# Two thirds of the expert slots placed ahead of the last four tiles' routing, which is cut into pieces and laid among them

## The chip, the cores and the metric

The kernel runs on one core of a Trainium2 chip, as one launch. The core has five instruction streams that run at the same time and meet only at semaphores: PE (matrix multiplication), DVE (vector work), ACT (activation functions and copies), POOL (slower vector work, and here the issue of every indirect DMA) and SP (issue of the plain DMAs). Each stream executes its own instructions strictly in order. The metric is the time of one execution in device microseconds (us); of a kernel's runs the median is taken.

## The reference, cut to what matters

A graph of 3,327 nodes with 256 features each (padded to 26 tiles of 128 rows) goes through two layers, every sublayer with a layer norm ahead of it and its result added to x:

```
x = x + gcn(norm(x), adj)          # normalized adjacency times a linear map
x = x + moe(norm(x))               # 8 experts, 2 chosen for each node
x = x + gat(norm(x), adj)          # attention over the graph
x = x + heads(norm(x))             # causal attention with 4 x 4 heads, gates, a small net
```

The change lies in the second line:

```
probs = softmax(tokens @ router_w.T);  rw, re = top_k(probs, 2);  rw = rw / sum(rw)
for e in range(8):
    h = gelu(tokens @ w1[e] + b1[e]);  y = h @ w2[e] + b2[e]
    out = out + combine[:, e:e+1] * y        # only the two chosen experts have a weight
```

## The kernel before, in words

All of it is float32 and written in Tile, a framework that puts instructions in each engine's stream and adds the semaphores. Most stages issue through `InOrder` (L42), a wrapper that keeps each engine's stream in the order in which the Python code makes the calls. Every wrapped call is recorded under line 53, so the profile shows L53 nearly everywhere and is read by tile names.

**The end of the first sublayer.** `graph0` (L151) sums neighbours in two parts. The first 16 row tiles are summed together, in 16 half banks of PSUM. The last ten (the loop over `i` from 16 to 25, L361 on) come one at a time: each takes 26 products of 128x128 by 128x256 in two halves of 13, each half with a panel of the adjacency matrix that SP loads, and ends with `gathered(i)`, a DVE instruction that adds the sum to `x`. After each half, `step(waiting)` (L37) moves every router generator that is under way on to its next `yield`.

**The router.** `Experts.route(tiles)` (L1329) is a generator for a group of tiles. In order it does: statistics of each tile on DVE (`rst`, `rmv`), their power of -0.5 on POOL (`rrs`); the normalized rows `tok` on DVE, and on POOL the sum of `x` and `tok` and a copy of each row's number; transposes on PE and their copy on ACT (`tokt`); logits on PE, softmax and the choice of two experts in some twenty small DVE instructions (`rm`, `rpr`, `ru`, `rat`, `chosen`), with one exponential on ACT; a copy of the first choice into `tok` on POOL; the choices `rsel`, which PE sums over the rows (`before`, `ones`); on DVE the rank of each row within its expert and the row's place in the table `places` in DRAM (`rplace`, which is made in place out of `rat`); and two *puts* per tile (L1437): indirect DMAs, issued by POOL, which scatter the 128 rows of a tile to their places. In the kernel before, tiles 0 to 15 go in four groups of four, tiles 16 to 23 in pairs, tiles 24 and 25 singly; after the last half a plain loop (L376) runs what is left of the generators.

**The experts.** `Experts.run` (L1450) puts 128 rows of zeros behind each expert's rows (8 more puts), then makes from the counts, on DVE, the tables of the 59 *slots*: slot i is 128 rows of one expert, and `row_i`, `exp_i` and `bias` tell which. 59 is what the worst routing needs (two choices times 26 tiles, and 7 for tiles that are not full). Then comes a loop over slots with three of them in work at a time: `take(i + 4)` (L1525) loads a slot's rows from `places` by a DMA of SP, at a row that SP reads from `row_i`; `turn(i)` (L1539) transposes them on PE and copies the expert's first weights and the transposed rows on DVE; `hidden(i - 1)` (L1565) has four products on PE and the gelu on ACT; `result(i - 2)` (L1581) has two products on PE, a DVE addition (`ye`) and a put that scatters the result rows into `made`. At i = 8 some weights for the next sublayer are made in between.

Three rules of order matter for what follows:

- `take` waits for all puts that have been issued by then and that no earlier `take` waited for (`self.puts`, L1529). The list holds the puts into `places` and those into `made`.
- Puts of one group (`places`, `made`) do not wait for each other, since their rows lie apart. A put into `places` is not freed in this way from loads that read `places`: Tile sees a write behind a read of the same tensor.
- POOL issues puts one after another, and everything else that POOL has to do stands in the same stream.

Of the kernel before, what the change touches and what calls it, by code (L numbers as in the profile page):

```python
# [2 lines left out]

# [33 lines left out]
def step(works):  # L37

    works[:] = [w for w in works if next(w, None) is None and w.gi_frame is not None]
# [54 lines left out]
class Net:  # L94
# [56 lines left out]
    def graph0(self, moe):  # L151
# [3 lines left out]
        with ExitStack() as ctx:  # L155
# [198 lines left out]
            moe.open(nc, ctx)  # L354
            coming = [moe.route(range(k, k + 4)) for k in range(0, NI, 4)]
            waiting = []
            H = NT // 2
            for i in range(NI, NT):
                acc = psa.tile([P, 2, D], F32, tag="acc", name="acc")
                for j0 in range(0, NT, H):  # L360
                    pan = panp.tile([P, NI, P], F32, tag="pan", name="pan")  # L361
                    nc.sync.dma_start(out=pan[:, :H, :], in_=a["adjt"][i][:, j0 : j0 + H, :])
                    for j in range(j0, j0 + H):
                        nc.tensor.matmul(
                            acc[:, 0, :], pan[:, j - j0, :], y[:, j, :, :P],
                            start=(j == 0), stop=(j == NT - 1),
                        )
                    if coming:
                        waiting.append(coming.pop(0))
                    step(waiting)  # L370
                gathered(i, acc[:, 0, :])
                if i in (17, 19, 21, 23):
                    coming.append(moe.route(range(i - 1, i + 1)))
                elif i > 23:
                    coming.append(moe.route(range(i, i + 1)))
            while coming or waiting:  # L376
                waiting += coming
                coming = []
                step(waiting)
# [863 lines left out]
class Experts:  # L1243
# [8 lines left out]

    SLOTS = 2 * NT + NE - 1
    ROOM = NP + P
# [54 lines left out]
    def open(self, nc, ctx):  # L1309

        self.nc, a = nc, self.a
        self.ps = ctx.enter_context(
            self.tc.tile_pool(name="mops", bufs=6, space=PSUM, reuse_waits="tile")
# [11 lines left out]

    def bank(self):
        return self.ps.tile([P, 2, D], F32, tag="r", name="rbank")

    def route(self, tiles):  # L1329
# [3 lines left out]
        mv = s.tile([P, 4, 2], F32, tag="rmv", name="rmv")[:, :n, :]  # L1333
        rs = s.tile([P, 4], F32, tag="rrs", name="rrs")[:, :n]
        for i, t in enumerate(tiles):
            st = s.tile([P, 6], F32, tag="rst", name="rst")
            nc.vector.bn_stats(st, x[:, t, :])
            nc.vector.bn_aggr(mv[:, i, :], st)
        nc.vector.tensor_scalar(rs, mv.rearrange("p t s -> p s t")[:, 1, :], 1e-5, None, ALU.add)
        nc.gpsimd.tensor_tensor(rs, rs, net.nhalf[:, :n], ALU.pow)  # L1340
        yield
        toks = []
        for i, t in enumerate(tiles):
            tok = s.tile([P, D + 2], F32, tag="tok", name="tok", bufs=20)
# [3 lines left out]
            toks.append(tok)  # L1348
        for t, tok in zip(tiles, toks):
            nc.gpsimd.tensor_tensor(x[:, t, :], x[:, t, :], tok[:, :D], ALU.add)  # L1350
            nc.gpsimd.tensor_copy(tok[:, D : D + 1], self.leave[:, t : t + 1])
        yield
# [11 lines left out]
        yield  # L1364
# [8 lines left out]
        m = s.tile([P, 4, 2], F32, tag="rm", name="rm")[:, :n, :]  # L1373
        pr = s.tile([P, 4, NE], F32, tag="rpr", name="rpr")[:, :n, :]
        u = s.tile([P, 4, NE], F32, tag="ru", name="ru")[:, :n, :]
# [4 lines left out]
        iota = self.iota.unsqueeze(1).to_broadcast([P, n, NE])  # L1380
        nc.vector.tensor_reduce(m[:, :, 0], pl, AX.X, ALU.max)
        nc.vector.tensor_tensor(pr, pl, wide(m[:, :, 0]), ALU.subtract)
        yield
        nc.scalar.activation(pr, pr, AF.Exp)
        yield
        nc.vector.tensor_reduce(m[:, :, 0], pr, AX.X, ALU.add)
        nc.vector.reciprocal(m[:, :, 0], m[:, :, 0])
        nc.vector.tensor_tensor(pr, pr, wide(m[:, :, 0]), ALU.mult)

        at = s.tile([P, 4, 2], F32, tag="rat", name="rat")[:, :n, :]  # L1390
        for k in range(2):
# [3 lines left out]
            nc.vector.scalar_tensor_tensor(u, u, float(NE), iota, ALU.mult, ALU.add)  # L1395
            nc.vector.tensor_reduce(at[:, :, k], u, AX.X, ALU.min)
            nc.vector.tensor_tensor(oh, iota, wide(at[:, :, k]), ALU.is_equal)
            if k == 0:
                nc.vector.scalar_tensor_tensor(pr, oh, -2.0, pr, ALU.mult, ALU.add)
        for i in range(n):  # L1400
            nc.gpsimd.tensor_copy(toks[i][:, D + 1 :], at[:, i, 0:1])
        sel = s.tile([P, 4, NE], F32, tag="rsel", name="rsel")[:, :n, :]
# [3 lines left out]
        w = s.tile([P, 4], F32, tag="rw", name="rw")[:, :n]  # L1406
        nc.vector.tensor_tensor(w, m[:, :, 0], m[:, :, 1], ALU.add)
        nc.vector.tensor_scalar(w, w, 1e-12, None, ALU.max)
        nc.vector.reciprocal(w, w)
# [3 lines left out]
        yield  # L1413
# [7 lines left out]
        whole = pc[:, 0, ds(n * NE, n * NE)].rearrange("p (t e) -> p t e", e=NE)  # L1421
        for i in range(n):
            nc.vector.tensor_tensor(u[:, i, :], above[:, i, :], self.count, ALU.add)
            nc.vector.tensor_tensor(self.count, self.count, whole[:, i, :], ALU.add)
        for k in range(2):
            nc.vector.tensor_tensor(pr, u, self.chosen[:, t0 : t0 + n, k, :], ALU.mult)
            nc.vector.tensor_reduce(self.rank[:, t0 : t0 + n, k], pr, AX.X, ALU.add)
        nc.vector.scalar_tensor_tensor(
            at, at, float(self.ROOM), self.rank[:, t0 : t0 + n, :], ALU.mult, ALU.add
        )  # L1430
        place = s.tile([P, 4, 2], I32, tag="rplace", name="rplace", bufs=8)[:, :n, :]
        nc.vector.tensor_copy(place, at)
        for i in range(n):
            for k in range(2):
                self.put(nc, place[:, i, k : k + 1], toks[i])

# [13 lines left out]
    def run(self, weights):  # L1450
        net, tc, S = self.net, self.tc, self.SLOTS
        nc = InOrder(tc)
        with ExitStack() as ctx:
            one = ctx.enter_context(tc.tile_pool(name="mor", bufs=1))
            wk = ctx.enter_context(tc.tile_pool(name="morw", bufs=4))
            ps = ctx.enter_context(tc.tile_pool(name="morps", bufs=8, space=PSUM))


            free = one.tile([P, NE], F32, name="free")
            free_i = one.tile([P, NE], I32, name="free_i")  # L1460
            nc.vector.tensor_tensor(free, self.spare, self.count, ALU.add)
            nc.vector.tensor_copy(free_i, free)
            for e in range(NE):
                self.put(nc, free_i[:, e : e + 1], self.zeros)


            past = one.tile([P, NE], F32, name="past")
            tiles_i = one.tile([P, NE], I32, name="tiles_i")
            nc.vector.tensor_scalar(past, self.count, float(P - 1), None, ALU.add)
            nc.vector.tensor_copy(tiles_i, past)  # L1470
            nc.vector.tensor_scalar(tiles_i, tiles_i, 7, None, ALU.arith_shift_right)
            tiles = one.tile([P, NE], F32, name="tiles")
            nc.vector.tensor_copy(tiles, tiles_i)
            nc.vector.tensor_copy(past, tiles)
            for e in range(1, NE):
                nc.vector.tensor_tensor(
                    past[:, e : e + 1], past[:, e : e + 1], past[:, e - 1 : e], ALU.add
                )
            first = one.tile([P, NE], F32, name="first")
            nc.vector.tensor_tensor(first, past, tiles, ALU.subtract)  # L1480

            def wide(v):
                return v.unsqueeze(1).to_broadcast([P, S, NE])

            slots = self.slots.unsqueeze(2).to_broadcast([P, S, NE])
            over = one.tile([P, S, NE], F32, name="over")
            has = one.tile([P, S, NE], F32, name="has")
            tmp = one.tile([P, S, NE], F32, name="tmp")
            nc.vector.tensor_tensor(over, slots, wide(past), ALU.is_ge)
            nc.vector.tensor_tensor(has, slots, wide(first), ALU.is_ge)  # L1490
            nc.vector.tensor_tensor(has, has, over, ALU.subtract)

            off = one.tile([P, NE], F32, name="off")
            nc.vector.tensor_scalar(off, self.iota, float(self.ROOM), None, ALU.mult)
            nc.vector.scalar_tensor_tensor(off, first, -float(P), off, ALU.mult, ALU.add)
            row = one.tile([P, S], F32, name="row")
            nc.vector.tensor_tensor(tmp, has, wide(off), ALU.mult)
            nc.vector.tensor_reduce(row, tmp, AX.X, ALU.add)
            nc.vector.scalar_tensor_tensor(row, self.slots, float(P), row, ALU.mult, ALU.add)

            none = one.tile([P, S], F32, name="none")
            nc.vector.tensor_scalar(
                none, self.slots, -float(P), self.count[:, 0:1], ALU.mult, ALU.add
            )
            nc.vector.tensor_tensor(none, none, over[:, :, NE - 1], ALU.mult)
            nc.vector.tensor_tensor(row, row, none, ALU.add)
            row_i = one.tile([P, S], I32, name="row_i")
            nc.vector.tensor_copy(row_i, row)
            exp = one.tile([P, S], F32, name="exp")
            nc.vector.tensor_reduce(exp, over, AX.X, ALU.add)  # L1510
            nc.vector.tensor_scalar(exp, exp, float(NE - 1), None, ALU.min)
            exp_i = one.tile([P, S], I32, name="exp_i")
            nc.vector.tensor_copy(exp_i, exp)
            bias = one.tile([P, 2, S], F32, name="bias")
            for f in range(2):
                nc.vector.tensor_tensor(tmp, has, wide(self.b1[:, :, f]), ALU.mult)
                nc.vector.tensor_reduce(bias[:, f, :], tmp, AX.X, ALU.add)

# [20 lines left out]
            def turn(i):  # L1539
                tok = took.pop(i)  # L1540
                pt = ps.tile([P, 2, D], F32, tag="b", name="pt")
# [166 lines left out]
```

## Time and profile before

| | us |
|---|---|
| median of three runs (3186.76, 3188.64, 3202.35) | 3188.64 |
| the profiled execution's own time | 3191.7 |
| its span, first to last instruction | 3189.9 |
| first 16 row tiles and all ahead of them | 0 to 278.85 |
| last ten row tiles, with the routing of most tiles | 278.85 to 427.15 |
| rest of the routing, zeros, tables | 427.15 to 466.77 |
| slots, up to the first use of their results | 466.77 to 599.4 |
| second layer: graph attention, heads | 599.4 to 3189.9 |

Within the span PE is busy for 2765.6 us (87%), DVE for 2557.9 (80%), ACT for 1638.0 (51%) and POOL for 891.4 (28%). The stage borders are read from the timeline: 278.85 is where the products of row tile 16 begin, 427.15 where those of tile 25 end, 466.77 the first transpose of a slot, 599.4 the first instruction that uses a result of the experts.

A line of the timeline gives the start, the busy time, the engine, the line of code, the operation with the tile that it writes and those that it reads, the shape and the count of merged instructions. In brackets stands how long the engine sat idle just before and what released it. A float32 product shows as two records, so a half of 13 products has x26. Lines with SPq or POOL and DMA in their names are the issue of a DMA, and the view of DMA issues gives the time from issue to landing.

### The profile page before, as it was taken

What the parts mean: (1) busy time and instruction counts of PE and PEld (TensorE: products, weight loads), DVE (VectorE), ACT (ScalarE), POOL (GpSimd) and SP (SyncE); (2) the same over time, 40 slices, a digit from 0 to 9 for tenths busy, and PEclk for the clock granted to TensorE, in tenths of its full rate; (3) what the DMA queues carried; (4) which work ended last, traced back from release to release, by engine and by line L of the source; (5) the groups of instructions that cost most, each with busy time, mean ns of one, the idle gap of its engine ahead of it and who ended that gap; (6) DMA issues with size and microseconds to landing.
All of it is one profiled execution on the core that took longest, in us unless ns stands there. A gap on an engine that the chain in (4) does not pass through costs nothing.

```text
span 3189.9 us, 126522 instructions
## 1 busy us (share of the span) xinstructions
PE 2765.6 (87%) x54266; PEld 2031.1 (64%) x54266; DVE 2557.9 (80%) x6460; ACT 1638.0 (51%) x4431; POOL 891.4 (28%) x1226
## 2 busy tenths in 40 slices
PE   5999859879887788998999899899998899989884
PEld 4788758757676666666666566555656565656553
DVE  4303457789997567999998998899999999999993
ACT  5410002555553445666655665556656556655663
POOL 3442545522123244432331221212111211111112
PEclk9999979989999789999999999999999999999996
DMA  9994524658673223333433333333333333433331
GB/s 342 337 302 136 160 75 122 229 201 287 230 259 111 62 65 88 104 95 98 110 104 89 102 110 95 100 103 106 107 113 100 107 103 109 114 102 105 109 104 53
DMA packets 248928, 434.31 MB, mean 136 GB/s; under 512 B 57872, under 2 KB 157712, under 8 KB 248240
## 3 DMA queue, kind: packets, MB, share of 16 engines
q1 hardware_dynamic: 231584, 400.24, 41.4%
q0 software_dynamic: 6960, 19.08, 1.6%
q8 instruction: 427, 7.00, 1.0%
q10 hardware_dynamic: 9824, 6.91, 0.7%
q14 instruction: 133, 1.09, 0.1%
HBM read 393.37 MB, written 25.88 MB: 131 GB/s over the span
## 4 chain that ended last, share of the span: by engine, by line
DVE 35%; PE 23%; ACT 3%; issue 2%; POOL 1%; DMA 1%; SPq 0%; POOLq 0%; DVEq 0%; ACTq 0%
DVE sc L53 31%; PE po L53 10%; PE pqk L53 8%; PE ptO L53 2%; ACT sc L53 2%; DMA vr<-vs 1%; PE pq L53 1%; DVE l2mv L53 0%; PE pt L53 0%; PE ph L53 0%; POOL fo L53 0%; DVE l1mv L53 0%; DVE gl L53 0%; DVE l2st L53 0%; DVE fo L53 0%
## 5 line engine op out<-in xcount | busy, mean ns | idle before, releaser
L53 ACT ACTIVATE sc<-sc,anmax 128x512 f32<-128x512 f32 (+3 forms) x1568 | 1041.4, 671 | 124.0 <-DVE anmax L53 123.8
L53 DVE TENSOR_SCALAR_CACHE_REDUCE sc<-pqk 128x512 f32<-128x512 f32 (+3 forms) x1568 | 898.6, 627 | 113.2 <-PE pqk L53 111.8
L53 PEld LDWEIGHTS po<-sc,vr 32*64 32x64 f32 x43728 | 678.8, 133 | 388.4 <-DVE sc L53 202.8
L53 PE MATMUL po<-sc,vr 32*64 32x128 f32 x43728 | 787.9, 280 | 136.0 <-DVE sc L53 57.5
L53 PE MATMUL pqk<-kt,qt 64*128 64x512 f32 (+3 forms) x3136 | 830.0, 584 | 57.7 <-DVE fo L53 19.9
L53 DVE STREAM_TRANSPOSE sc<-sc 128x2048 f32<-128x2048 f32 (+3 forms) x392 | 815.9, 2082 | 15.1 <-ACT sc L53 15.0
L53 PEld LDWEIGHTS pqk<-kt,qt 64*128 64x128 f32 x3136 | 319.3, 188 | 294.2 <-issue 114.5
L53 PE MATMUL acc<-wh,p 128*128 128x259 f32 x1352 | 309.8, 387 | 33.8 <-DVE p L53 33.7
L53 POOL TENSOR_TENSOR ot<-ot,sxd 128x512 f32<-128x512 f32 x104 | 132.7, 1276 | 705.0 <-ACT ot L53 673.7
L53 PEld LDWEIGHTS acc<-wh,p 128*128 128x128 f32 x1352 | 254.0, 190 | 91.8 <-DVE p L53 51.3
L53 ACT ACTIVATION_READ_ACCUMULATOR sc<-sc,anmax 128x1 f32 x1568 | 303.9, 194 | 0.0
L53 PE MATMUL acc<-y,pan 128*128 128x256 f32 x1352 | 302.1, 386 | 1.7 <-issue 1.7
L53 PEld LDWEIGHTS acc<-y,pan 128*128 128x128 f32 x1352 | 260.8, 194 | 39.6 <-issue 2.8
L53 ACT ACTIVATE u<-u,d 128x512 f32<-128x512 f32 (+1 forms) x182 | 125.2, 688 | 157.1 <-DVE u L53 157.0
L53 ACT COPY qkv<-ptO 128x256 f32<-128x256 f32 x104 | 38.7, 372 | 278.1 <-PE ptO L53 278.1
L53 DVE SCALAR_TENSOR_TENSOR u<-bc,d 128x512 f32<-128x512 f32 (+1 forms) x182 | 136.3, 749 | 0.1
L53 DVE SCALAR_TENSOR_TENSOR p<-pan,u 128x512 f32<-128x512 f32 (+1 forms) x182 | 126.0, 693 | 10.5 <-PE acc L53 6.1
L53 PE MATMUL ptO<-igw,ot 128*128 128x68 f32 x832 | 119.6, 288 | 13.2 <-DVE sc L53 4.4
L53 DVE DVE_READ_ACCUMULATOR sc<-pqk 128x1 f32 x1568 | 129.5, 83 | 0.0
L53 PEld LDWEIGHTS ptO<-igw,ot 128*128 128x128 f32 x832 | 104.9, 197 | 32.9 <-issue 23.0
L53 ACT COPY tokt<-rbank 128x512 f32<-128x512 f32 (+1 forms) x14 | 7.4, 557 | 200.1 <-PE rbank L53 200.1
L53 POOL TENSOR_TENSOR qkv<-qkv,gss 128x1024 f32<-128x1024 f32 x26 | 50.0, 1924 | 211.0 <-DVE gss L53 180.5
(283 smaller groups left out, 3005.1 us busy)
## 6 DMA issues: line engine op xcount, KB each, us to landing
vr<-vs SPq DMA_DIRECT2D x1248, 128.0 KB, 2.7
ar<-in_adj_dram SPq DMA_DIRECT2D x104, 832.0 KB, 7.5
pan<-in_adjt_dram SPq DMA_DIRECT2D x156, 256.0 KB, 4.4
pan<-in_adjt_dram SPq DMA_DIRECT2D x26, 1024.0 KB, 9.1
pan<-in_adjt_dram SPq DMA_DIRECT2D x20, 832.0 KB, 4.6
vr<-vs SPq DMA_DIRECT2D x96, 96.0 KB, 2.2
took<-places SPq DMA_DIRECT2D x59, 129.0 KB, 2.2
vr<-vs SPq DMA_DIRECT2D x112, 64.0 KB, 2.0
```

The source lines that it names most:

```text
L53: made = make(*args, **kw)
```

## The change

The routing groups become larger, and the slots are put in two parts.

- While the last ten row tiles are summed, only tiles 0 to 21 are routed: 0 to 7 from the first half on, 8 to 15 from the fourth, 16 to 19 from the ninth, 20 and 21 from the thirteenth. The steps of one group follow half upon half; the second group starts in the half in which the first issues its puts, and its calls stand behind them. Up to now the stages of several groups stood side by side.
- From the 17th half on, `table()` makes the tables of the first 37 slots (`SURE`). Whatever the routing, the tokens of 22 tiles fill at least 37 slots of 128 rows. These need no zeros.
- `run` starts with these slots. Tiles 22 to 25 are routed as one group, and then `table(last=True)` issues the zeros and makes the tables of the other 22 slots. This work is cut at every `yield 0`, and two pieces are laid behind each slot's step. Two puts of a tile are one piece, and each put of zeros is one.
- The copy of the first choice into `tok` moves from POOL to ACT, and so does the copy of the transposed rows in `turn` from DVE to ACT.
- The slots' PSUM tiles come from the router's pool of 6 banks (before: 8 of their own), `tok` has 18 buffers (before: 20), and the weights for the next sublayer are made at i = 41 (before: 8).

The diff, cut to its core:

```diff
-def step(works):
-    works[:] = [w for w in works if next(w, None) is None and w.gi_frame is not None]
+def step(works, small=False):
+    left = []
+    for w in works:
+        for end in w:
+            if end or small:
+                left.append(w)
+                break
+    works[:] = left
...
-            coming = [moe.route(range(k, k + 4)) for k in range(0, NI, 4)]
+            begun = {
+                0: lambda: moe.route(range(0, 8)),
+                3: lambda: moe.route(range(8, NI)),
+                8: lambda: moe.route(range(NI, NI + 4)),
+                12: lambda: moe.route(range(NI + 4, NI + 6)),
+                16: moe.table,
+            }
...
-                    if coming:
-                        waiting.append(coming.pop(0))
+                    k = 2 * (i - NI) + h
+                    if k in begun:
+                        waiting.append(begun[k]())
                     step(waiting)
...
     SLOTS = 2 * NT + NE - 1
+    EARLY = NT - 4
+    SURE = (2 * P * EARLY - NE * (P - 1) + P - 1) // P
...
             nc.vector.bn_aggr(mv[:, i, :], st)
+            yield 0
...
-            tok = s.tile([P, D + 2], F32, tag="tok", name="tok", bufs=20)
+            tok = s.tile([P, D + 2], F32, tag="tok", name="tok", bufs=18)
...
         for i in range(n):
-            nc.gpsimd.tensor_copy(toks[i][:, D + 1 :], at[:, i, 0:1])
+            nc.scalar.copy(toks[i][:, D + 1 :], at[:, i, 0:1])
...
         for i in range(n):
+            yield 0
             for k in range(2):
                 self.put(nc, place[:, i, k : k + 1], toks[i])
+
+    def table(self, last=False):
+        nc = self.nc
+        lo, hi = (self.SURE, self.SLOTS) if last else (0, self.SURE)
...
+            for e in range(NE):
+                yield 0
+                self.put(nc, free_i[:, e : e + 1], self.zeros)
...
-        nc = InOrder(tc)
+        nc = self.nc
...
-                nc.vector.tensor_copy(tt.rearrange("p k q -> p (k q)"), pt[:, 0, :])
+                nc.scalar.copy(tt.rearrange("p k q -> p (k q)"), pt[:, 0, :])
...
             for i in range(4):
                 take(i)
+            rest = [chain(self.route(range(self.EARLY, NT)), self.table(last=True))]
             for i in range(S + 2):
+                if i + 4 == self.SURE:
+                    while rest:
+                        step(rest)
                 if i + 4 < S:
                     take(i + 4)
...
                     result(i - 2)
-                if i == 8:
-                    weights(nc, lambda: ps.tile([P, 2, D], F32, tag="b", name="pv"))
+                for _ in range(2):
+                    step(rest, small=True)
+                if i == self.SURE + 4:
+                    weights(nc, self.bank)
```

## The prediction

> **What bounds the kernel now.** I read the busy table, then the stretches by stage, then the timeline of the two stretches that the change touches, then the waits, and last the times from DMA issue to landing.
>
> ```profile
> 278.85:427.15 148.30, 138.12 (x691) 121.28 (x689) 71.51 (x329) 7.90 (x19) 72.64 (x121) 0.95 0.42 136
> 427.15:466.77 39.62, 7.15 (x33) 5.94 (x32) 25.85 (x131) 1.38 (x5) 21.01 (x29) 0.53 0.19 65
> 466.77:599.40 132.63, 123.00 (x830) 112.45 (x830) 93.49 (x367) 38.02 (x119) 62.99 (x61) 0.95 0.41 121
> ```
>
> The columns are length, busy time of PE, PEld, DVE, ACT and POOL, granted PE clock, DMA share, GB/s. PE bounds the last ten row tiles (138 of 148 us) and the slots (123 of 133). Between them lies a gap of 39.6 us in which PE works for 7: the rest of the routing, the zeros and the tables. The slots repeat every 1.975 us with PE always busy. The second layer, 2590 us, is left alone.
>
> ```profile
> 461.00 0.96 POOL L53 DMA_INDIRECT places<-zeros,free_i  x1 [0.30 <-issue]
> 466.77 0.45 PE L53 MATMUL pt<-ident,took 128*128 128x128 f32 x1 [19.38 <-DMA took<-places]
> ```
>
> The first line is the last put ahead of the slots. The first load was issued at 464.48, so from the start of a put to the load that waits for it takes 3.48 us, and from the load to the transpose 2.3.
>
> ```profile
> took<-places SPq DMA_DIRECT2D x59, 129.0 KB, 2.2
> made<-ye,at_to POOLq DMA_INDIRECT x59, 2.6
> places<-tok,rplace POOLq DMA_INDIRECT x52, 2.8
> ```
>
> These are medians from issue to landing. Puts in a row stand 1.27 us apart (0.96 busy, 0.30 between them).
>
> ```profile
> 352.47 0.96 POOL L53 DMA_INDIRECT places<-tok,rplace  x1 [0.30 <-issue]
> 353.43 0.53 POOL L53 COPY tok<-rat 128x1 f32<-128x1 f32 x4
> 354.00 0.17 DVE L53 SCALAR_TENSOR_TENSOR rat<-rat,rank 128x8 f32<-128x8 f32 x1 [4.32 <-POOL tok L53]
> ```
>
> This shows what a row of puts does to POOL's other work: a copy stands behind them, and DVE idles 4.32 us for it. PE pays too:
>
> ```profile
> PE rbank L53 <- DVE rw L53: 7.0, 2, 3.5
> PE rbank L53 <- DVE rsel L53: 3.2, 1, 3.2
> ```
>
> That is 10.2 us of PE idle time in the first stretch, all of it; after each of the three waits 26 product records took 7.26 to 7.79 us instead of 5.79, 5.2 us more in all.
>
> **What the change removes.** The gap: 39.6 us. Tables and loads of the first slots are ready before the last product, so the first transposes follow it at once. In the first stretch the copy moved to ACT takes the three waits away (10.2 and 5.2), and the products of tiles 22 and 23 leave for the slots (1.7). Together 17.1 there, if nothing new were late.
>
> **What it adds, first stretch.** In the compiled order of POOL the 16 puts of tiles 0 to 7 stand ahead of the power (`rrs`) of tiles 8 to 15. DVE's next eight `tok` wait for that power, and PE's next 16 transposes for the `tok`. Worked out from rows of before: tiles 0 to 7 begin on DVE at 280.4; eight statistics at 0.53, the power (0.55 for one column, 0.72 for two, 1.04 for four: 1.65 for eight), eight `tok` at 0.59 end at 291.5, the transposes at 292.0. A half of 13 products (5.7) and logits (1.85 for four tiles, 3.75 for eight) end at 301.5. The choice is 18 instructions of some 0.25 and an exponential, over at 306.4, before PE comes for it at 307.2; the sums end at 307.9. Ranks are 22 small instructions, 4.6 us: the puts start at 312.7 and end 16 times 1.27 later, at 333.1. The power ends at 334.9 and the last `tok` at 339.7. PE, a half later at 313.6, wanted to transpose until 315.4 and ends at 340.0: **24.6 us of idle time**. The same sum for tiles 16 to 19, whose power stands behind the second 16 puts (363.2 to 383.6), gives 11.0, and for 20 and 21, behind eight puts, 3.2. With about 5 us for the slow clock after three long waits (the 5.2 above) this adds 38.8 + 5. Less the 17.1, the stretch grows by 27 and ends near 454. Bounds: 22 (no slow clock, POOL's power hidden) to 32 (10 for the clock).
>
> [...]
>
> **What it adds, slots.** Up to slot 14 the four tiles' routing goes along. DVE gets 11.9 us (2.1 statistics, 2.3 `tok`, 4.7 choice, 2.8 ranks and places) and later 7.5 for the tables, in 25 steps; a step leaves it 0.33 idle, and 0.4 more with the copy on ACT, so 18 us fit if spread evenly, but pieces of five or six instructions (1.0 to 1.3) don't. It also waits for POOL's power once (1 to 2) and for an exponential that now stands between gelus, with a table load ahead of it and one behind (1.28 each in the trace; one such load is shown). PE gets 3.4 us of products. I take 8 for all of it; bounds 3 (PE's part, the rest hidden) and 14 (everything that exceeds the slack, serial).
>
> Then comes a wait that before does not have. In the compiled waits, each put into `places` from step 14 on waits for the newest load from `places` (step 14's for load 18, step 15's for load 19, and so on to step 19's for load 23), and each load waits for the puts of the step before. Put and load thus take turns: load to put 2.3 us, last put to load 2.7 (a put of `made`, 541.73, let the load of 544.82 go 3.1 later) to 3.48, and 1.27 for each further put. I take 2.9. Two steps with four puts: 2.3 + 2.9 + 3.8 = 9.0 each. Four steps with two zeros: 2.3 + 2.9 + 1.3 = 6.5. In all 44.0, and with 2.3 ahead of the first put and what follows it, load 24 lands 50.2 us after slot 14's transpose. In the regular beat slot 24 comes after 19.75. So PE **stands 30 us**. Queued behind a waiting put on POOL are the puts of results, for which the loads wait as well, but they are issued while the loads are under way. Bounds: 24 (2.2 and 2.0, the shortest landings) and 36 (3.48 each, and POOL late). After it PE's clock costs 2 (0 to 2), by the 1.5 to 2 us above.
>
> The sum is −39.6 + 27 + 8 + 30 + 2 = **+27.4**. Against the profiled execution's 3191.7 that is 3219; it lies 3.1 above the median, so on that scale **3216**, with bounds of +9.4 and +44.4, 3198 to 3233. Moving the copy of `turn` to ACT costs nothing: ACT has 0.62 us per step, 1.0 with it. If PE did not set the beat it would show as a wait for `turned`. The later weights cost what they cost now (slots 8 to 11 took 12.6 us, 6.7 more than three beats).
>
> **The rivals.**
>
> *It does what it says.* POOL's queue delays nothing and puts don't wait for loads: −17.1 − 39.6 + 10 = −46.7, 3142. For it: the gap is real and its work fits. Against it: 1.27 us per put, and the compiled waits. It decides where 16 puts take less than a half's 5.7 us, under 0.36 each, and a put goes without its load.
>
> *Only the first queue.* Puts in the slots run beside the loads, POOL's power is late as above: 27 − 39.6 + 10 = −2.6, 3186, not slower. The mechanism is that loads are four slots ahead: a load goes out 4.0 us after a transpose and lands at 6.2, against 7.9 for the need, so 1.7 us of lateness are free. It decides if a put's wait is for a load long landed. The compiled waits name the newest one, which speaks against it.
>
> *Only the second.* POOL's power comes in time, or PE has slack: −17.1 − 39.6 + 40 = −16.7, 3172, or 3189 if the old waits stay as well. Against it: POOL's order.
>
> *Worse.* Each turn of put and load costs half as much again (places landed after up to 6.0 us), 46, and DVE falls behind by 20: 27 − 39.6 + 20 + 46 + 5 = +58, 3247.
>
> **How the numbers follow.** Forecast 0.70, it does what it says 0.06, only the first 0.09, only the second 0.08, worse 0.07. The likeliest case gives 3216. The range has to take in 0.8: the forecast's own bounds, 3198 to 3233, hold about 0.66; down to 3184 come the first rival with one queue (0.09) and half of the other (0.04), up to 3236 a little of the worst. What this kernel's measurement tells from no change is about 0.5%, 16 us. Faster by more: 0.06 and half of the 0.08, 0.10. Within: 0.09, the other 0.04 and the forecast's low tail 0.05, 0.18. Slower: 0.72.
>
> **What would show it.** In the changed profile, the gap at PE between the last product and the first transpose of a slot is under 3 us. DVE's `tok` wait for POOL's `rrs` by about 18 us once, and PE's `rbank` for DVE's `tok` by 25, 11 and 3. Products of the row tiles end near 454. In the slots, PE's transposes wait for `took` six times in a row, 9 and then 6.5 us apart, near 485 to 530, while POOL's puts wait for the DMA of `took`. The slots' results are first used near 627. It would be wrong if the first wait of PE were under 10 us (POOL's order costs less than its rows), if the loads kept their beat of 2 us through steps 14 to 19, or if the second layer's time moved by more than a few us, of which I know no reason.

## The result: about one per cent slower, by the two queues that were forecast

The changed kernel takes 3225.86 us in the median of six runs (3216.92 to 3240.38); the kernel before, run beside it, takes 3195.0. The ratio is 1.0102, with a 95% interval of 1.0072 to 1.0133: 23 to 42 us slower. The forecast was +27.4 us and 3216. The profiled execution of the changed kernel took 3240.4 us and is the slowest of the six, so its stages are compared one by one and checked with a second profile below. Its span is 3238.5.

The first view is the table of stretches, with the same columns and borders as before the change: row tiles 16 to 25, the gap behind them, the slots, the second layer.

```profile
286.30:468.85 182.55, 144.87 (x672) 123.51 (x670) 66.70 (x264) 9.67 (x37) 67.55 (x92) 0.85 0.34 112
468.85:471.75 2.90, 0.00 (x1) 0.03 (x1) 1.14 (x4) 0.00 (x0) 0.00 (x0) 1.00 0.23 56
471.75:650.16 178.41, 139.08 (x858) 122.56 (x858) 92.29 (x390) 63.78 (x187) 81.73 (x87) 0.88 0.34 102
650.16:3238.50 2588.34, 2270.75 (x51624) 1595.98 (x51624) 2297.20 (x5431) 1494.13 (x4156) 639.69 (x786) 0.95 0.41 120
```

| stretch | before | after | difference | forecast |
|---|---|---|---|---|
| up to row tile 16 | 278.85 | 286.3 | +7.5 | 0 |
| row tiles 16 to 25 | 148.3 | 182.55 | +34.2 | +27 |
| gap | 39.6 | 2.9 | −36.7 | −39.6 |
| slots | 132.6 | 178.4 | +45.8 | +40 |
| second layer | 2590.5 | 2588.3 | −2.2 | 0 |
| sum | 3189.9 | 3238.5 | +48.6 | +27.4 |

The 48.6 us lie between two single executions; the medians differ by 30.9. Where the rest went is taken up under e6 and in the section on the prediction.

Two things are to be seen. In the slots PE was busy for 123 of 133 us and is now busy for 139 of 178: it no longer sets the beat. And its granted clock fell from 0.95 to 0.85 in the row tiles and to 0.88 in the slots.

**The gap.** The last product ends at 468.85. What is left of the gap is one wait:

```profile
471.75 0.41 PE L60 MATMUL rbank<-ident,took 128*128 128x128 f32 x2 [2.90 <-DMA took<-places]
```

**Row tiles.** This is the timeline of POOL, DVE and PE where PE waits longest, and under it all waits of PE in the stretch (waiter, for whom, total, times, longest).

```profile
341.02 0.96 POOL L60 DMA_INDIRECT places<-tok,rplace  x1 [0.30 <-issue]
342.29 0.96 POOL L60 DMA_INDIRECT places<-tok,rplace  x1 [0.30 <-issue]
343.27 1.69 POOL L60 TENSOR_TENSOR rrs<-rrs,nhalf 128x8 f32<-128x8 f32 x1
345.00 2.36 DVE L60 TENSOR_SCALAR tok<-x,rmv,rrs 128x256 f32<-128x256 f32 x4 [18.55 <-issue]
345.56 1.72 PE L60 MATMUL rbank<-ident,tok 128*128 128x128 f32 x6 [22.45 <-DVE tok L60]
```

```profile
PE rbank L60 <- DVE tok L60: 27.0, 5, 22.4
PE rbank L60 <- issue: 10.2, 1, 10.2
```

The row of 16 puts runs from 323.00 to 343.25, 1.27 us apart. The power of tiles 8 to 15 follows it without a pause, DVE's `tok` follows the power, and PE's transposes the first `tok`. DVE has idled 18.55 us for it and PE 22.45. The second line is the same wait for tiles 16 to 19; the view has lost its releaser's name, but in the timeline the power ends at 397.81 behind another 16 puts, `tok` starts at 397.85 and PE at 398.41.

**Slots.** PE and POOL in turn, between 523 and 541:

```profile
523.70 0.66 PE L60 MATMUL rbank<-ident,took 128*128 128x128 f32 x2 [5.83 <-DMA took<-places]
524.36 0.95 POOL L60 DMA_INDIRECT places<-tok,rplace  x1 [3.34 <-DMA took<-places]
533.27 0.66 PE L60 MATMUL rbank<-ident,took 128*128 128x128 f32 x2 [5.50 <-DMA took<-places]
533.91 0.96 POOL L60 DMA_INDIRECT places<-zeros,free  x1 [3.35 <-DMA took<-places]
540.77 0.66 PE L60 MATMUL rbank<-ident,took 128*128 128x128 f32 x2 [3.42 <-DMA took<-places]
```

The first put of a turn waits for a load, and the transpose waits for the same load. The next load has waited for the puts; SP's waits between 440 and 660 us have these two lines:

```profile
SPq L60 <- DMA places<-zeros,free: 15.2, 6, 5.4
SPq L60 <- DMA places<-tok,rplace: 9.8, 2, 8.4
```

In these turns a load goes out 2.7 to 3.4 us after the start of the last put into `places`, and a put 2.8 to 2.9 us after the load. The six transposes stand 9.57, 7.50, 6.94, 7.05 and 7.51 us apart instead of 1.975. Behind them the products of `w` and `h` take 1.55 to 1.91 us instead of 1.03, with a granted clock of 0.50 in the first five of them and of 0.66 in the last.

### The profile page after: what moved, and what is told of

The parts are those of the page before. It is cut to its first block, busy times and chain, and to the rows that moved or that the text cites. A ratio compares the mean times of both kernels' runs of the same rounds, so it can differ in the third digit from the quotient of the medians.

```text
span 3238.5 us, 126539 instructions
## 1 busy us (share of the span) xinstructions
PE 2795.6 (86%) x54246; PEld 2048.7 (63%) x54246; DVE 2525.3 (78%) x6291; ACT 1664.2 (51%) x4512; POOL 885.0 (27%) x1195
## 4 chain that ended last, share of the span: by engine, by line
DVE 39%; PE 24%; ACT 2%; issue 2%; POOL 1%; DMA 1%; SPq 0%; ACTq 0%; POOLq 0%; DVEq 0%
DVE sc L60 34%; PE po L60 9%; PE pqk L60 8%; PE ptO L60 2%; PE acc L60 2%; ACT sc L60 1%; PE pq L60 1%; DVE l2mv L60 1%; PE psxt L60 1%; PE pt L60 0%; DVE l1mv L60 0%; DMA vr<-vs 0%; DVE gl L60 0%; DVE l2st L60 0%; PE ph L60 0%
## 5 line engine op out<-in xcount | busy, mean ns | idle before, releaser
L60 PE MATMUL pqk<-kt,qt 64*128 64x512 f32 (+3 forms) x3136 | 841.4, 588 | 55.9 <-DVE fo L60 20.1
L60 DVE STREAM_TRANSPOSE sc<-sc 128x2048 f32<-128x2048 f32 (+3 forms) x392 | 816.0, 2082 | 10.4 <-ACT sc L60 10.3
L60 ACT ACTIVATE junk<-ar 128x1664 bf16<-128x1664 f32 x52 | 82.7, 1591 | 52.9 <-DMA ar<-in_adj_dram 52.4
```

The source lines that it names most:

```text
L60: made = make(*args, **kw)
```

## The experiments

The theory is that of the prediction: POOL's order holds the row tiles, and turns of put and load hold the slots. The first rival to it is that the larger groups' own work on DVE holds the row tiles; the second, that POOL's 1.27 us per put hold the slots, whatever the loads do. The table has the stages of every profile, cut at three marks that all kernels have: DVE's first use of the first 16 row tiles' sums, the first transpose of a slot, the first use of the slots' results.

| kernel | to first sums | to first slot | slots | rest | profiled span |
|---|---|---|---|---|---|
| before | 273.5 | 193.3 | 132.6 | 2590.5 | 3189.9 |
| changed | 281.0 | 190.8 | 178.4 | 2588.3 | 3238.5 |
| r1 changed again | 280.1 | 190.8 | 177.2 | 2571.1 | 3219.2 |
| e1 newer first | 277.1 | 174.2 | 175.4 | 2571.4 | 3198.1 |
| e2 puts spread | 278.7 | 150.5 | 176.8 | 2580.8 | 3186.7 |
| e3 loads free | 278.0 | 191.3 | 163.4 | 2573.1 | 3205.8 |
| e4 both mended | 278.0 | 145.2 | 150.9 | 2585.8 | 3159.9 |
| e5 before, choice on ACT | 272.7 | 185.7 | 132.5 | 2587.0 | 3177.8 |
| e6 before, turn on ACT | 275.6 | 193.4 | 130.0 | 2577.4 | 3176.4 |
| e7 changed, padded | 273.8 | 188.8 | 174.9 | 2572.1 | 3209.5 |
| e8 before, shifted | 279.4 | 193.5 | 130.9 | 2588.4 | 3192.2 |
| e9 mended, padded | 274.1 | 147.5 | 145.5 | 2573.8 | 3140.9 |
| e10 logits halved | 273.4 | 148.3 | 155.1 | 2570.6 | 3147.4 |

### r1: the changed kernel once more

> The changed kernel once more, unchanged, for a second profile. Its first profile took 3240.4 us, 14.5 above its median, and in it the first 16 row tiles alone, which the change does not touch, ended 7.5 us later than before. Theory (the loss lies in POOL's queue during the last ten row tiles and in the turns of put and load in the slots): the three waits of PE for tok come back at 22, 10 and 4 us within 3, the six waits for took at 29 within 3, and the first 16 row tiles end within 3 us of where they ended before. Rival (the long panel stage is chance): these waits differ by more than 5 us from profile to profile.

PE's three waits came at 22.5, 10.3 and 3.7 us and those for `took` at 27.6 in all (28.7 in the first profile), so the two mechanisms are no chance. But the first sums were used at 280.1 again, 6.6 us later than before the change: the theory missed this, and e7 and e8 follow it up. The second layer took 17 us less than in the first profile, with the same instructions; a difference of that size between two single profiles says nothing of a change. What the medians say of it stands under e6.

### e1: the newer group's step first

```diff
-    for w in works:
+    for w in reversed(works):
         for end in w:
...
-    works[:] = left
+    works[:] = left[::-1]
```

> Within a half the newer group's step is called first, so the power of tiles 8 to 15 stands ahead of the 16 puts of tiles 0 to 7; but now 32 puts instead of 16 and 16 stand in a row ahead of the power of tiles 16 to 19. Theory (POOL's order sets PE's waits): the first wait of PE for tok falls from 22.4 to under 6 us, the second grows from 10 to some 20 (32 puts of 1.27 are 40.6 us), the third stays near 4; the row tiles' stage changes by less than 8 us. Rival (the waits come from the eight-tile groups' own work on DVE, whatever POOL does): the first wait stays above 15 us and the second near 10.

The power of tiles 8 to 15 stands ahead of all puts, 32 puts stand ahead of the next. The waits of PE:

```profile
PE rbank L60 <- issue: 16.2, 1, 16.2
PE rbank L60 <- DVE tok L60: 4.9, 4, 3.7
PE acc L60 <- issue: 2.6, 3, 1.0
```

The first wait fell from 22.4 to under 1, the second grew from 10.2 to 16.2, the third stayed at 3.7. The wait moves with the place of the power in POOL's stream, and DVE's work is the same in both kernels: the first rival falls. The size was off: the stage lost 17 us, not under 8. The slow clock behind the first wait went with it: the half there took 5.79 us instead of 7.01.

### e2: the puts spread over the halves

As e1, and besides:

```diff
-            nc.gpsimd.tensor_copy(tok[:, D : D + 1], self.leave[:, t : t + 1])
...
         for i in range(n):
-            yield 0
+            yield int(i > 0)
+            nc.gpsimd.tensor_copy(toks[i][:, D : D + 1], self.leave[:, t0 + i : t0 + i + 1])
```

> As the run with the newer group first, and the puts of a tile are issued one tile in each half, each behind the copy of its rows' numbers, which keeps them from being drawn forward; 0, 14 and 30 puts stand ahead of the three later powers, spread over the halves. Theory: all three waits of PE for tok fall to a sum under 10 us (from 36), the slow products behind them go too, and the kernel gains 30 to 40 us over the changed one: 3186 to 3196, about level with before. Rival (DVE's larger groups are the cause): the waits stay above 20 us in sum and the gain is under 12.

```profile
PE rbank L60 <- DVE tok L60: 6.2, 8, 3.8
```

The waits fell from 37.2 us in all to 6.2, and the stage from 190.8 to 150.5, 40 us, of which 31 are waits and the rest is clock (the halves behind the first two waits take 5.79 us instead of 7.01 and 7.92). The median is 3186.3; the ratio to before is 0.9982 (0.9963 to 1.0002). The first queue is settled: with it mended and the second left, the kernel is level with before.

### e3: loads that puts do not wait for

```diff
+                if 0 < i < self.SURE:
+                    tc.declare_no_dep(made.ins, group="places", reason="rows apart")
+                    tc.add_to_no_dep_group("places", made.ins)
-                while self.puts:
+                while self.puts and (i == 0 or i >= self.SURE):
                     tc.add_manual_dep(
```

> Loads of slots 1 to 36 neither wait for the last four tiles' puts and the zeros nor are waited for by them: these rows lie behind the full slots, and slot 37's load waits for all puts. POOL's order is left as it is. Theory (turns of put and load cost the slots 30 to 36 us): the six waits of PE for took, 29 us, vanish; what is left is POOL's queue of 16 more puts, 20 us of it in six slots, of which the four buffers for results and POOL's free time hide 8 to 12, so 8 to 12 us of idle time come in their place; gain over the changed kernel 20 to 28 us, 3198 to 3206. Rival (POOL's puts at 1.27 us each are what holds the slots, not the loads): gain under 8 us, with the same idle time at PE under another name.

The six waits for `took` (25.1 us) went and the slots fell from 178 to 163.4, 14 to 15 us instead of 20 to 28; the ratio to before is 1.0065 (1.0043 to 1.0088). So the turns of put and load are real, but more came in their place than the 8 to 12 us that I had for POOL's queue. This is the timeline of PE, ACT, DVE and POOL in that stretch; "remote" is a semaphore update that the trace ties to no instruction.

```profile
513.50 1.62 PE L60 MATMUL rbank<-turned,w1e 128*128 128x128 f32 x8 [2.08 <-DVE w1e L60]
...
517.30 0.96 POOL L60 DMA_INDIRECT made<-ye,at_to  x1 [0.30 <-issue]
518.56 0.96 POOL L60 DMA_INDIRECT places<-tok,rplace  x1 [0.30 <-issue]
519.59 0.62 ACT L60 ACTIVATE h<-rbank,bias 128x128 f32<-128x128 f32 x2 [6.14 <-remote]
...
520.00 2.07 PE L60 MATMUL rbank<-w,h 128*128 x4 [4.88 <-issue]
...
525.18 0.42 DVE L60 TENSOR_TENSOR ye<-rbank,b 128x256 f32<-128x256 f32 x1 [11.67 <-remote]
```

The products end at 515.12 by their records, and the gelu that needs them starts at 519.59; those of 520.00 end at 522.07, and the addition that needs them starts at 525.18. Neither engine has other work. With 1.6 us at 513.08 before, some 9 us are spent in this way while POOL issues puts one behind another. What makes PE's completions late is open; more of it below.

### e4: both mended

The edits of e2 and e3, and the last four tiles' puts and the zeros kept in a list, one of which is issued behind each slot; results get 8 buffers.

```diff
+                if self.later:
+                    self.put(nc, *self.later.pop(0))
...
-                y = wk.tile([P, D], F32, tag="y", name="ye")
+                y = wk.tile([P, D], F32, tag="y", name="ye", bufs=8)
```

> The spread puts of the second experiment and the free loads of the third together; besides, the last four tiles' puts and the zeros are issued one behind each slot instead of two to four, and the results have 8 buffers instead of 4. Theory (both queues were the loss): row tiles' stage as with the spread puts, 150 us from the first use of the sums to the first slot; slots 132.6 of before, 8 of crowding, 3 for the clock and at most 5 for POOL's two puts per slot (2.5 us against a beat of 2.0, hidden by the buffers); 40 us under the changed kernel's slots with free loads left out of account: 3145 to 3160 in all, 30 to 45 under before. Rival (a row of puts holds PE back whatever else is mended, since PE's completions came up to 5.6 us late in rows of more than ten puts in the runs so far): 16 slots of puts without a pause cost 15 us or more, 3165 to 3180.

3156.8 us, ratio 0.991 (0.9891 to 0.993): within the theory's range, below the rival's. With both queues mended the kernel gains 30 us; the rival by which the change does what it says had 47. The slots still take 150.9 us, 18 more than before, and one wait in them is of the old kind, slot 37 for the last zeros:

```profile
PE rbank L60 <- DMA took<-places: 4.8, 2, 4.6
```

### e5: the first choice's copy on ACT, in the kernel before

```diff
-            nc.gpsimd.tensor_copy(toks[i][:, D + 1 :], at[:, i, 0:1])
+            nc.scalar.copy(toks[i][:, D + 1 :], at[:, i, 0:1])
```

> The kernel before, with nothing but the copy of the first choice into tok moved from POOL to ACT. Theory (as in the prediction: that copy stands behind puts on POOL, and DVE and PE wait for it): the three waits of PE, 10.2 us, and the slow products after them, 5.2, go: the stage of the last ten row tiles falls from 148.3 to 132 to 135, the whole by 13 to 17. Rival (the rest of POOL's queue, the powers and the sums, holds DVE as well): the waits stay under another name, the whole falls by less than 6. It also shows how long the first 16 row tiles take in a kernel without the change, 273.5 us in the one profile of it.

The three waits of 3.2 to 3.5 us fell to two of 0.8 and 1.4, and a new one came:

```profile
362.54 1.12 PE L53 MATMUL rbank<-ident,tok 128*128 128x128 f32 x4 [5.46 <-DVE tok L53]
```

The stage got 7.6 us shorter, half of what I had claimed, and the whole did not move beyond its interval (0.9995, 0.9979 to 1.0011). The copy was one thing that stood behind puts on POOL; with it gone the power behind them is the next that PE waits for, as the rival had it. The prediction's 15.4 us for this edit by itself were wrong. In the changed kernel the grouping had moved the waits already.

### e6: the transposed rows' copy on ACT, in the kernel before

```diff
-                nc.vector.tensor_copy(tt.rearrange("p k q -> p (k q)"), pt[:, 0, :])
+                nc.scalar.copy(tt.rearrange("p k q -> p (k q)"), pt[:, 0, :])
```

> The kernel before, with nothing but the copy of the transposed rows in a slot moved from DVE to ACT. Theory: no change beyond 3 us, since PE sets the beat of 1.975 us and ACT has 0.62 us of work in it, 1.0 with the copy. Rival: PE waits for the copy behind the gelu, the beat grows by 0.1 us or more, 6 us or more over 59 slots.

The beat stayed at 1.975 us, so the rival falls. The ratio is 0.9969 (0.9953 to 0.9985), 5 to 15 us faster. The profile shows 2.6 us of this in the slots, at their start and at the weights. So the theory holds for the beat, but not for the whole kernel: the rest lies in a stage that the edit does not touch, the second layer.

The medians point to the same stage in all kernels. Take from each kernel's median the 1.9 us that its runs have outside the span, and its profiled time up to the slots' results (in the two profiles of the changed kernel this differs by 2.1 us). What is left is an estimate of the second layer: 2586 to 2594 us for the kernel before in its five sets of runs, 2590 for e5, 2576 for e6, and 2571 to 2581 for the changed kernel and all that were made from it. These last have the copy of `turn` on ACT as well. So about 10 us of the second layer go with this copy, the only thing that e6 changes; how it acts on instructions that stand far behind it is open.

### e7 and e8: where the buffers lie

All changed kernels up to e4 used the first sums 4 to 8 us later than before, though up to there they issue the same loads and products. The compiled programs differ in addresses: new tiles and two `tok` buffers fewer moved the panels by 832 bytes. e7 adds an unused tile of 320 bytes per partition to the changed kernel, e8 one of 192 bytes to the kernel before.

```diff
         self.rank = one.tile([P, NT, 2], F32, name="rank")
+        self.pad = one.tile([P, 80], F32, name="pad")
```

> The changed kernel with an unused tile of 320 bytes per partition ahead of the first sublayer's buffers, so that these start at a multiple of 512 bytes again, as in the kernel before (by the compiled programs the panels lie at 148480 there, 147648 after the change, 147968 here). All four changed kernels so far began to use the first sums at 277.1 to 281.0 us, the three without the change at 272.7 to 275.6, and moved 358 to 359 GB/s between 124 and 184 us, against 379 to 387. Theory (the new tiles moved the buffers that the panels and rows are loaded into, and loads to the moved ones are slower): 380 GB/s come back, the first sums are used at 273 to 275, PE's wait of 2.7 us for a panel goes, and the kernel gains 4 to 6 us. Rival (it is chance or another part of the change): 359 GB/s stay.

> The kernel before with an unused tile of 192 bytes per partition at the same place, so that the panels lie 192 bytes beyond a multiple of 512, as after the change. Theory: between 124 and 184 us it moves 355 to 362 GB/s instead of 383, PE waits once for a panel near 220 us, and the first sums are used at 277 to 281. Rival: nothing of this; 383 and 273.

The same stretch of 60 us in four kernels (last column GB/s, the one before it the DMA engines' share). Before:

```profile
124.00:184.00 60.00, 60.00 (x280) 52.82 (x279) 9.26 (x18) 27.75 (x33) 28.14 (x68) 1.00 1.06 383
```

Changed:

```profile
124.00:184.00 60.00, 60.00 (x280) 52.81 (x279) 8.22 (x16) 25.38 (x32) 25.83 (x64) 1.00 1.10 359
```

Changed, padded (e7):

```profile
124.00:184.00 60.00, 60.00 (x280) 52.92 (x279) 9.26 (x18) 28.26 (x33) 28.14 (x68) 1.00 1.07 388
```

Before, shifted (e8):

```profile
124.00:184.00 60.00, 60.00 (x280) 52.91 (x279) 8.23 (x16) 26.12 (x31) 25.94 (x64) 1.00 1.09 360
```

In the two of these four kernels whose panels lie 192 bytes beyond a multiple of 512, the same loads ran at 359 and 360 GB/s against 388 and 383 in their counterparts, 7.5 and 6.0% slower, with the DMA engines busier (1.10 and 1.09 against 1.07 and 1.06). PE waited for a panel there, 2.7 us in the changed kernel and 5.0 in e8, and in e7 and in the kernel before not at all. The first sums follow: 273.8 in e7, 279.4 in e8. e7's ratio to before is 1.0086 (1.0063 to 1.0108). The intervals of 1.0102 and 1.0086 overlap, so that the 5 us stand on the profiles. What moved is the side that the loads write, and no run tells of which multiple the distance counts. The unused tile moves the other buffers of the first sublayer with the panels, so which of them counts is not told apart either.

### e9: both mended, padded, and the last routing in denser pieces

The edits of e4, the tile of e7, and three pieces behind each slot instead of two.

> Both queues mended as in the fourth experiment, the unused tile of 320 bytes, and three pieces of the last routing behind each slot instead of two, so that its puts start four or five slots earlier. Theory: 4 to 6 us from the panels' place; of the 4.6 us that slot 37 waited for the last zeros, and of 2 us of slow products behind it, most goes, while denser pieces cost DVE 1 to 3: 3145 to 3152, against 3157. Rival (denser pieces cost what the earlier puts save, and the panels' place nothing): 3155 to 3160.

3145.9 us, ratio 0.9865 (0.9844 to 0.9885), as the theory had it. This is the fastest version, 45 us under before. The slots take 145.5, and slot 37's wait fell from 4.6 us to 2.5, less than the theory had:

```profile
509.36 0.66 PE L60 MATMUL rbank<-ident,took 128*128 128x128 f32 x2 [2.48 <-DMA took<-places]
```

Up to the slots' results this kernel takes 567.1 us, 32.3 less than before; the other 13 of the 45 are, by the estimate under e6, the shorter second layer.

### e10: the logits of a group in two halves

In e9 no wait of PE in the row tiles is over 0.5 us, and yet its halves are uneven. The stretches of a group's logits, 16 products or 32 records in a row, and of the 4 us behind them:

```profile
298.54:303.00 4.46, 4.46 (x34) 4.45 (x32) 0.00 (x0) 0.00 (x0) 0.00 (x0) 0.78 0.55 195
303.00:307.00 4.00, 4.00 (x11) 3.19 (x12) 3.10 (x14) 1.10 (x9) 0.00 (x0) 0.50 0.00 0
```

PE is busy all the time, and its clock is 0.50 behind the logits. e10 issues them four tiles in each of two halves:

```diff
                     pl[:, i, :], turned[i][:, k, :], self.rwt[:, k, :], start=(k == 0), stop=(k == 1)
                 )
+            if i == 3 and n == 8:
+                yield 1
```

> The kernel of the ninth experiment, with the logits of an eight-tile group issued four tiles in one half and four in the next. In that experiment the 32 logits products of 8 columns each stood in a row for 4.6 us without a pause, and the clock granted to PE was 0.50 for 6.8 us from their middle on, so that the half behind them took 8.26 us instead of 5.79, twice; 16 such products in a row, 1.85 us, left it at 1.00. Theory (it is the row of narrow products, although PE counts as busy): 1.85 us of logits in each of four halves, the clock at 1.00 all through, no half above 5.9 us: the row tiles' stage falls by 5 to 7 us, the whole to 3139 to 3142. Rival (the clock falls for the larger group's other work, or by chance): the halves behind the logits stay above 7 us, the whole within 2 us of 3146.

```profile
297.85:299.55 1.70, 1.70 (x17) 1.70 (x16) 1.16 (x3) 0.00 (x0) 1.17 (x2) 1.00 0.39 63
299.55:305.26 5.71, 5.71 (x28) 5.02 (x28) 3.96 (x6) 0.00 (x0) 5.37 (x9) 1.00 0.33 133
```

The clock stays at 1.00 and the halves behind logits take 5.87 us, as the theory of the narrow row has it. The kernel gained nothing by it: 3149.5, ratio 0.9873 (0.9833 to 0.9914). The puts now come later and stand ahead of the power of tiles 20 and 21, for which PE waits 6.43 us and then runs slowly (7.27 us for the next half instead of 5.79). One reason is the split, another that DVE began on the sums of tiles 16 to 19 5.0 us after their recorded end. And the slots took 155.1 us instead of 145.5, with late completions as in e3 (the addition at 479.54 starts 4.3 us after the recorded end of its products), though their instructions stand in the same order on POOL. My expected total was wrong by these two.

## Why the prediction was right, and where it was not

**The gap** was to vanish but for 3 us: it fell from 39.6 to 2.9.

**POOL's queue in the row tiles** was worked out as 24.6, 11.0 and 3.2 us of waits. Measured: 22.45 with 0.55 more behind it, 10.17 and 3.65. e1 and e2 show that the puts ahead of the power are the cause.

**The slow clock in the row tiles was mis-sized**: 5 us in the prediction, 14 measured. The stretch of 182.55 has 37.2 of waits; without its own waits, its slow products and two tiles, the stretch before the change would be 148.3 − 10.2 − 5.2 − 1.7 = 131.2; 182.55 − 37.2 − 131.2 leaves 14.1. I took the 5.2 us of three waits of 3 us as the price of three waits of any length. Some 10 lie behind the waits: after the wait of 22 us alone the transposes took 3.7 us more than 1.8 and the next half 7.01 instead of 5.79. Some 5 lie at the eight-tile logits, which took 3.65 and 4.59 us and had halves of 7.53 and 8.25 behind them: e9 and e10 show that these slowed PE with no wait at all (8.26 us in e9, 5.87 with the logits halved in e10). The prediction had eight-tile logits at twice the price of four-tile ones and nothing for the clock.

**The crowding of DVE and PE** was taken as 8 us. Slots 0 to 14 took 35.06 us against 14 beats, 27.65, and slots 14 to 18 took 8.92 against 7.90: 8.4 in all.

**The turns of put and load** were taken as 30 us, with 2 for the clock. From slot 18 to 24 PE took 46.5 us against 11.85, 34.7 more, and up to slot 41 another 2.8: 37.5 against 32. The mechanism is that of the prediction, load 24 coming 55.5 us after slot 14 instead of 50.2. The turn with two zeros was the one taken too short, 6.9 to 7.5 us instead of 6.5: from a load to the put that waits for it the sum had 2.3 us, and it took 2.8 to 2.9. The rival, that POOL's puts alone cost the slots, may keep a part: e4, with free loads and the puts one by one, still has 18 of the 45.8 us, and no run tells how much of that is POOL's.

**The copy of `turn` and the later weights** were costed at nothing. The weights cost 6.4 us beyond the beat, as before (6.7). The beat did not change in e6; that the whole kernel got faster with the copy on ACT was not foreseen.

**What was not seen at all** is the 5 us ahead of the stage. The sum treated everything up to row tile 16 as untouched, because its instructions are; e7 and e8 show that its buffers were moved. With this and the clock the products of the row tiles ended at 468.85 us instead of near 454.

**The second layer** was to stay within a few us, and a larger move was named as a sign of being wrong. In the first profile it moved by 2.2, but from profile to profile it scatters from 2571 to 2590, and by the medians it got 12 to 20 us shorter (the estimate under e6). I had put this at nothing.

So the sign and both mechanisms are as forecast, but that the size came out so close, 30.9 us for 27.4, is partly luck. The terms left out (5 for addresses, 9 of the clock, 5 for the turns and 3 for what is left of the gap) would have made the sum 49, and up to the slots' results the two profiles of the changed kernel do lose 50.8 and 48.7 us. In the medians the shorter second layer took most of that excess back.

Three of the rivals were brought about by experiments. "Only the second" is e2: 3186.3, where the prediction had 3172 to 3189. "Only the first" is e3: 3210.8, where the prediction had 3186; it allowed 10 us for the slots, and they took 31 more than before. "It does what it says" had 3142: e4 reaches 3156.8, and e9, with the buffers' place mended too and the help of the second layer, 3145.9.

## What to carry to other kernels

Before work is moved into larger groups, write out each in-order queue as it will stand: here a power of 1.7 us stood behind 16 puts, 1.27 us apart, and for it DVE stood idle for 18.55 us and PE for 22.45. Before work is laid among loads, look at which tensor it writes: a write that must wait for the newest read, and a read that must wait for the newest write, made a chain of round trips here, with slots 6.9 to 9.6 us apart instead of 1.975, though the loads were meant to be four slots ahead. And compare the addresses of what is loaded, not only the instructions, ahead of the place that was changed: here 192 bytes came with 360 GB/s instead of 383.

## What the runs showed of the hardware that was not expected

**A row of narrow products slowed PE's clock.** 16 products (32 records) that each move 8 columns, 4.5 us in a row, brought the granted clock to 0.50 for 6.8 us by the trace's clock records, from 301.0 and again from 328.3 in e9 (0.78 in the mean from 298.54 to 303.00, 0.50 to 307.00, 0.90 to 311.10), and the 26 product records behind them to 8.26 us instead of 5.79. In e10 eight of them in a row (16 records), 1.85 us, left it at 1.00. In e9 the clock fell while PE counts as busy throughout, 4.46 of 4.46 us in the logits: the trace, in which the ends of products are modelled, shows PE idle nowhere there.

**Loads into buffers 192 bytes beyond a multiple of 512 ran 6.0 and 7.5% slower** (360 and 359 GB/s against 383 and 388), in both directions of the test.

**PE's completions reached other engines late in six of the profiles.** In the changed kernel, r1, e1, e2, e3 and e10, while POOL issued puts one behind another, engines that waited for PE alone started 1.6 to 9.2 us after the products' recorded end: a panel load of SP 5.7 us in the changed kernel and 4.2 in r1, DVE's first use of a group's sums 9.2 in e1, where PE itself stopped three times (the 2.6 us for `acc`), and 5.0 in e10. In e4, e7 and e9, with rows as long, none did by over 0.6 us, so a row of puts is not enough to bring it about. Whether the products or their signals were late the trace cannot tell, because the ends of products in it are modelled. No run brings it about by itself, and the cause stays open.
